# Turning the attention of a graph layer without TensorE: blocks of 32 on VectorE and a trip through DRAM

## The chip, the cores and the metric

The kernel runs on one core of a Trainium2 chip. The metric is the device time of one execution in microseconds (us). Before the change it is 2218.47 us, the median of three runs from 2218.12 to 2219.33 us. The profile is that of one execution with a span of 2214.6 us.

The engines that matter are TensorE (PE in the profile; PEld is its loading of weights), VectorE (DVE), ScalarE (ACT), GpSimd (POOL) and SyncE (SP), which here issues nearly all transfers. Each works through its own list of instructions in order, and waits on semaphores for the others.

## The reference

`x` has 128 batches of 128 nodes with 512 features, all float32. Four layers follow each other, each of the form `x = layernorm(x + layer(x))`. `adj` is a 128x128 weighted adjacency.

```python
# layer 0
y = einsum('nm,bmd->bnd', adj, x) @ weight + bias
# layer 1
rel = adj.T * (x Wq^T)(x Wk^T)^T
rel = rel / norm(rel, axis=2)
y = rel @ (x Wv^T)
# layer 2
h = x @ W
e = leaky_relu(s1[:, :, None] + s2[:, None, :], 0.2) * adj   # s1 = h a1, s2 = h a2
att = softmax(e, axis=2)
y = elu(att @ h + beta * h)
# layer 3
A = adj @ x;  C = adj @ x + b
y = max over the last axis of relu(A[:, :, None, :] + (C - A)[:, :, :, None])
```

The change concerns layer 2. There `att @ h + beta * h` is `(att + beta I) @ x @ W`, and this is how the kernel computes it: it needs the transpose of `att + beta I` as an operand of TensorE.

## The kernel before, in words

The 128 batches are worked in 32 groups (`NG`) of four (`G`). A tile of a group has 128 partitions (nodes) and 4x512 elements. Every matmul is in float32.

**Order of the work.** Each layer is cut into small pieces, and each piece is recorded with a due time by `emit(at, f)`. `TABLE` gives the due times of a group in slots; group g adds 28 slots for each group before it. At the end all pieces are sorted by due time and written out, and `InOrder` makes the framework keep this order on each engine. So four groups are in work at a time: while layer 2 of group g runs, layer 1 works on group g+1, layer 0 on group g+2, and the end of layer 2 and layer 3 on group g-1. `FIRST` and `LAST` give other times for the first two and the last three groups. Every instruction goes through the helper in line 26, so that the profile puts all of them on L26; they are told apart by their tiles.

**Products with weights.** The four products with 512x512 weights (tiles r_y, r_m, r_v, r_z for layers 0, 1, 1 and 2) are done as seven smaller products instead of eight, with sums of blocks. `product` emits them in the order 1, 2, 6, 5, 7, 3, 4, one slot apart, and for each an eviction 0.72 slots later. In the text they are called the first to the seventh product by this order. They share three regions of PSUM:

```python
ORDER = (1, 2, 6, 5, 7, 3, 4)
REGION = {1: 0, 6: 0, 7: 0, 4: 0, 2: 1, 5: 2, 3: 2}
```

A product that follows in the same region adds onto what stands there, after the earlier one has been read out. So the sixth product (number 3) waits for the eviction of the fourth (number 5), and the seventh (number 4) for that of the fifth (number 7). In layer 0 all seven evictions are VectorE additions onto x: `x<-r_y,x` in the profile.

**The attention of layer 2.** For a group: `spread` puts s2 along rows by TensorE, `leaky` adds s1 and applies the leaky ReLU on VectorE, `weighted` multiplies by `adj` on GpSimd, `greatest` takes the maximum on VectorE, `exps` does the exponentials with their sums on ScalarE. Then come the steps that the change touches:

- `divide` takes the reciprocals `rs` of the sums on VectorE, and multiplies the tile `e` (128 x 4 x 128) by them, on GpSimd where the whole group is done at once. In the last group, which goes batch by batch, it is on VectorE.
- `turn_att` turns the four 128x128 blocks on TensorE into the PSUM tile p_eT.
- `with_beta` adds beta times the identity (`beta_i`) on VectorE and writes the tile `eT`.
- `gather` multiplies x2 with `eT` on TensorE: p_z, copied to `zT` by ScalarE.

By the table `divide` is due at slot 65.8, `turn_att` at 68.6, `with_beta` at 69.0 and `gather` from 71.5 on. In the same slots VectorE has the fourth product's eviction of layer 0 for group g+2 (slot 66.72 in the count of group g), the variance `ve` of layer 2's norm of group g-1, its `nmean`, the fifth product's eviction, the masking of layer 1's scores (`rel`), and their turning in blocks (`relB`).

**Other turns without TensorE.** Layer 1 turns x (from group 2 on) and rel in blocks of 32x32 on VectorE (`turn_blocks`, `turn_rel`: tiles xB, relB) and then moves the blocks to their places by transfers from SBUF to SBUF, 16 a group each (`move`, `move_rel`: tiles xT, relT). They are all issued on SyncE's queue, in order, as are the loads of x and the stores of the result.

Of the kernel before, what the change touches and what calls it, by code (L numbers as in the profile page):

```python
# [8 lines left out]
FP = mybir.dt.float32  # L9
AF = mybir.ActivationFunctionType  # L10
ALU = mybir.AluOpType
# [18 lines left out]
def kernel(  # L30
# [33 lines left out]
    pe, dve, act, pool = (InOrder(tc, e) for e in (nc.tensor, nc.vector, nc.scalar, nc.gpsimd))  # L64
    sync = InOrder(tc, nc.sync)
    B, N, D = x.shape
    P = 128
    assert N == P and D % P == 0
    K = D // P
    Q = P // 32  # L70
    H = D // 2
    G = 4
    NG = B // G
# [4 lines left out]
    work = ctx.enter_context(tc.tile_pool(name="work", bufs=1))  # L78
    small = ctx.enter_context(tc.tile_pool(name="small", bufs=4))
    psum = ctx.enter_context(tc.tile_pool(name="psum", bufs=1, space=bass.MemoryType.PSUM))  # L80

    def bank(name):
        return psum.tile([P, D], FP, tag="ps", name=name, bufs=3)
# [56 lines left out]
    beta_i = const.tile([P, P], FP)  # L140
# [79 lines left out]
    def emit(at, f, *args):  # L220
        pieces.append((at, lambda: f(*args)))

    def each(at, f):
        for b in range(len(at)):
            emit(at[b], f, b)

    def row(at, step, n=G):
        return [at + i * step for i in range(n)]
# [6 lines left out]
        move=row(20.5, 0.1), x_sums=row(25.3, 0.5), m=row(28, 1, 7), scores=row(36.5, 1),  # L235
# [2 lines left out]
        residual=row(51.0, 1), dots=[51.7, 53.8, 54.9, 55.6], norm1=[54.6], scale=[57.2],  # L238
        apply1=row(65.4, 0.33),
        spread=[61.6], leaky=[62.0], weighted=[63.4], greatest=[64.3], exps=[64.4],  # L240
        divide=[65.8], turn_att=[68.6], with_beta=[69.0], gather=row(71.5, 1),
        z_sums=row(75.3, 0.5), z_w=row(77, 1, 7), exp=[87.5, 88.5, 90.4, 92.0],
        elu=[87.8, 89.4, 92.8, 93.8], norm2=[95.0], apply2=row(95.7, 0.33),
        widen=[98.7, 100.0, 103.6, 104.6], top=[99.1, 100.4, 104.0, 105.0],
# [14 lines left out]
            gather=row(36.7, 0.9), z_sums=row(39.95, 1.3),  # L259
# [6 lines left out]
            m=[0.0, 1.73, 3.46, 5.2, 7.4, 9.1, 10.8], scores=row(12.7, 0.9), masked=[16.4],  # L266
# [4 lines left out]
            turn_att=row(54.4, 0.6), with_beta=row(54.9, 0.6), gather=[55.2, 56.1, 60.5, 65.0],  # L271
# [98 lines left out]
    def rows_of(t):  # L370
        return lambda nh, ch: t()[:, 2 * nh : 2 * nh + 2, H * ch : H * ch + H]


    def stats(s, g, b, t):
        if b == 0:
            s["mv"] = small.tile([P, G, 2], FP, tag="mv", name=f"mv_{g}", bufs=6)
        st = small.tile([P, 6], FP, tag="st", name=f"st_{g}_{b}")
        dve.bn_stats(st, t)
        dve.bn_aggr(s["mv"][:, b, :], st)
# [239 lines left out]

    def layer2(g, t):  # L620
        s = {}

        def spread():
            s["p"] = bank(f"p_s2_{g}")
            for b in range(G):
                pe.transpose(
                    s["p"][:, b * P : (b + 1) * P],
                    s12[g][:, 1, b : b + 1].to_broadcast([P, P]),
                    ident,
                )  # L630

        def leaky():
            e = work.tile([P, G, P], FP, tag="e", name=f"e_{g}")
            dve.tensor_tensor(
                e,
                s["p"].rearrange("p (b n) -> p b n", b=G),
                s12[g][:, 0, :, None].to_broadcast([P, G, P]),
                ALU.add,
            )
            dve.scalar_tensor_tensor(e, e, ALPHA, e, op0=ALU.mult, op1=ALU.max)  # L640
            s["e"] = e

        def weighted():
            pool.tensor_tensor(s["e"], s["e"], adj_b, ALU.mult)

        def greatest():
            s["nm"] = small.tile([P, G], FP, tag="nm", name=f"nm_{g}")
            dve.tensor_reduce(s["nm"], s["e"], AX.X, ALU.max, negate=True)

        def exps(i):  # L650
            if i == 0:
                s["sums"] = small.tile([P, G], FP, tag="sums", name=f"sums_{g}")
            for b in range(i * n, i * n + n):
                act.activation(
                    s["e"][:, b, :],
                    s["e"][:, b, :],
                    AF.Exp,
                    bias=s["nm"][:, b : b + 1],
                    accum_out=s["sums"][:, b : b + 1],
                )  # L660

        def divide(i):
            rs = small.tile([P, n], FP, tag=f"rs{n}", name=f"rs_{g}_{i}")
            dve.reciprocal(rs, s["sums"][:, i * n : i * n + n])
            e = s["e"][:, i * n : i * n + n, :]
            engine = pool if n == G else dve
            engine.tensor_tensor(e, e, rs[:, :, None].to_broadcast([P, n, P]), ALU.mult)

        def turn_att(i):
            if i == 0:  # L670
                s["p"] = bank(f"p_eT_{g}")
            for b in range(i * n, i * n + n):
                pe.transpose(s["p"][:, b * P : (b + 1) * P], s["e"][:, b, :], ident)

        def with_beta(i):
            if i == 0:
                s["eT"] = work.tile([P, G, P], FP, tag="eT", name=f"eT_{g}")
            dve.tensor_tensor(
                s["eT"][:, i * n : i * n + n, :],
                s["p"].rearrange("p (b n) -> p b n", b=G)[:, i * n : i * n + n, :],  # L680
                beta_b[:, i * n : i * n + n, :],
                ALU.add,
            )

        def gather(b):
            if b == 0:
                s["zT"] = work.tile([P, K, G * P], FP, tag="aT_yz", name=f"zT_{g}")
            p = bank(f"p_z_{g}_{b}")
            for k in range(K):
                pe.matmul(  # L690
                    p[:, k * P : (k + 1) * P],
                    x2[g][:, b, k * P : (k + 1) * P],
                    s["eT"][:, b, :],
                    start=True,
                    stop=True,
                )
            act.copy(
                s["zT"][:, :, b * P : (b + 1) * P], p.rearrange("p (k n) -> p k n", k=K)
            )

        def begin():
            s["c"] = work.tile([P, G, D], FP, tag="c", name=f"c_{g}")
            for b in range(G):
                s["c", b] = s["c"][:, b, :]

        def direct(b):

            s["c", b] = psum.tile([P, D], FP, tag="r0", name=f"c_{g}_{b}", bufs=2)
            for k in range(K):
                pe.matmul(  # L710
                    s["c", b],
                    s["zT"][:, k, b * P : (b + 1) * P],
                    w2_sb[:, k, :],
                    start=(k == 0),
                    stop=(k == K - 1),
                )

        def exp(b):
            s["m", b] = work.tile([P, D], FP, tag="m", name=f"m_{g}_{b}", bufs=3)
            act.activation(s["m", b], s["c", b], AF.Exp)  # L720

        def elu(b):
            if b == 0:
                x3[g] = data.tile([P, G, D], FP, tag="x3", name=f"x3_{g}")
            x = x3[g][:, b, :]
            dve.scalar_tensor_tensor(
                x, s["c", b], 0.0, x2[g][:, b, :], op0=ALU.max, op1=ALU.add
            )
            dve.scalar_tensor_tensor(x, s["m", b], 1.0, x, op0=ALU.min, op1=ALU.add)
            stats(s, f"2_{g}", b, x)  # L730

        n = G // len(t["exps"])
        emit(t["spread"][0], spread)
        emit(t["leaky"][0], leaky)
        emit(t["weighted"][0], weighted)
        emit(t["greatest"][0], greatest)
        each(t["exps"], exps)
        each(t["divide"], divide)
        each(t["turn_att"], turn_att)
        each(t["with_beta"], with_beta)  # L740
        each(t["gather"], gather)
        if g < NG - 1:
            left_factors(t["z_sums"], s, "zT", "s_yz", f"z_{g}", 0)
            product(t["z_w"], f"z_{g}", by_rows, s, "2", rows_of(lambda: s["c"]), True, begin)
        else:
            each(t["z_w"], direct)
        each(t["exp"], exp)
        each(t["elu"], elu)
        norm(t["norm2"], t["apply2"], s, f"2_{g}", lambda: x3[g])
# [73 lines left out]
    for g in range(NG):  # L823
        for layer in (layer0, layer1, layer2, layer3):
            layer(g, times(g))
# [31 lines left out]
```

## Time and profile before

| what | value |
|---|---|
| time, median of 3 | 2218.47 us |
| span of the profiled execution | 2214.6 us |
| TensorE busy, matmuls | 2170.9 us (98%) |
| VectorE busy | 1547.9 us (70%) |
| ScalarE busy | 1102.5 us (50%) |
| GpSimd busy | 907.7 us (41%) |
| transpose of the attention on TensorE, p_eT | 128 instructions, 273 ns recorded each |
| adding beta, eT | 31 of 128x512, 674 ns each, and 4 of 128x128 |
| dividing on GpSimd, e by rs | 31, 1039 ns each |
| moves of rel, SBUF to SBUF | 512 issues, 16 KB each, 1.8 us to landing |

A busy time is the sum over an engine's instructions. Recorded matmuls overlap: the next begins before the record of the last ends, so the time that a matmul really holds TensorE is read from start to start, or from the chain of waits. On VectorE, too, an instruction that doesn't need the result of the one ahead starts a little before the record of that one ends. In a timeline a line has start, duration (both in us), engine, source line, operation, output and inputs; a bracket at its end gives how long the engine stood idle before it, and what released it.

### The profile page before, as it was taken

The page shows a single profiled execution, that of the slowest core. Times are in us where ns is not written, and L with a number is a line of the kernel's source. Part 1 is how long each engine was busy: PE and PEld are TensorE (multiplying, and loading weights), DVE is VectorE, ACT ScalarE, POOL GpSimd, SP SyncE. Part 2 cuts the span into 40 slices and gives each one's busy share as a digit, 9 for nine tenths or more (in the row PEclk, how much of TensorE's full clock was granted, in tenths as well). Part 3 has the DMA queues.
Part 4 walks back from the last instruction along what each step waited for, and adds up shares of the span by engine and source line. Part 5 has one row for each costly group of instructions (what it writes and reads, how often), then busy time and mean ns, then how long its engine had stood idle before and what let it go on. Part 6 is the DMA issues. An engine that isn't in the chain of part 4 may idle for free.

```text
span 2214.6 us, 31863 instructions
## 1 busy us (share of the span) xinstructions
PE 2170.9 (98%) x11073; PEld 1839.6 (83%) x11073; DVE 1547.9 (70%) x3290; ACT 1102.5 (50%) x2446; POOL 907.7 (41%) x743
## 2 busy tenths in 40 slices
PE   7999999999999999999999999999999999999996
PEld 5788888888888888888888888888888888888873
DVE  4657766767766767776767776767767677667676
ACT  2224445554445554445554445554455554455547
POOL 3334444334444344443344443344443344443321
PEclk9999999999999999999999999999999999999998
DMA  4011222211222211222112222112222112221101
GB/s 167 25 20 29 61 60 62 62 20 49 60 60 63 58 21 52 59 61 62 44 31 56 58 62 63 41 30 59 58 62 63 29 39 62 59 63 44 21 28 57
DMA packets 333295, 115.15 MB, mean 52 GB/s; under 512 B 297424, under 2 KB 297552, under 8 KB 333136
## 3 DMA queue, kind: packets, MB, share of 16 engines
q1 hardware_dynamic: 331936, 110.77, 19.7%
q10 hardware_dynamic: 1200, 2.36, 0.3%
q8 instruction: 88, 1.44, 0.3%
q14 instruction: 71, 0.58, 0.1%
HBM read 39.65 MB, written 33.55 MB: 33 GB/s over the span
## 4 chain that ended last, share of the span: by engine, by line
PE 93%; DVE 3%; ACT 2%; POOL 1%; issue 1%; DMA 0%; ACTq 0%; DVEq 0%; POOLq 0%
PE r_y L26 17%; PE r_v L26 17%; PE r_m L26 17%; PE r_z L26 17%; PE p_z L26 5%; PE p_rel L26 5%; PE p_y L26 5%; PE p_o L26 5%; PE p_a L26 5%; DVE x L26 1%; ACT x L26 1%; DVE st L26 1%; PE p_eT L26 1%; PE p_m L26 1%; PE p_s L26 1%
## 5 line engine op out<-in xcount | busy, mean ns | idle before, releaser
L26 ACT ACTIVATE x<-x,nmean,rstd 128x512 f32<-128x512 f32 x384 | 288.6, 808 | 120.8 <-DVE nmean L26 120.8
L26 DVE BATCH_NORM_STATS2 st<-x 128x6 f32<-128x512 f32 x384 | 263.8, 687 | 8.8
L26 POOL TENSOR_TENSOR x<-x,bias_sb 128x512 f32<-128x512 f32 x128 | 170.1, 1331 | 137.9 <-PE p_y L26 137.5
L26 DVE SCALAR_TENSOR_TENSOR x<-m,x 128x512 f32<-128x512 f32 x128 | 114.4, 894 | 108.5 <-ACT m L26 98.5
L26 POOL TENSOR_TENSOR s_x<-xT 128x512 f32<-128x512 f32 x64 | 82.2, 1285 | 261.1 <-DMA xT<-xB 250.2
L26 ACT COPY c<-r_z 128x512 f32<-128x512 f32 x124 | 71.2, 574 | 223.3 <-PE r_z L26 198.0
L26 ACT COPY yT<-p_y 128x512 f32<-128x512 f32 x128 | 75.1, 586 | 213.6 <-PE p_y L26 213.6
L26 POOL TENSOR_TENSOR rstd<-ve,mhalf 128x4 f32<-128x4 f32 (+1 forms) x99 | 98.5, 995 | 194.1 <-DVE ve L26 188.9
L26 DVE TENSOR_TENSOR x<-r_y,x 128x512 f32<-128x512 f32 x224 | 151.7, 678 | 31.2 <-PE r_y L26 31.0
L26 DVE SCALAR_TENSOR_TENSOR scr<-x,wa 128x512 f32<-128x512 f32 x256 | 161.5, 675 | 0.0
L26 DVE STREAM_TRANSPOSE xB<-x 128x512 f32<-128x512 f32 x120 | 81.2, 696 | 108.7 <-ACT x L26 97.7
L26 PEld LDWEIGHTS p_y<-adjT,x 128*128 128x128 f32 x1024 | 136.9, 196 | 11.2 <-ACT adjT L26 4.8
L26 POOL TENSOR_TENSOR s_z<-zT 128x512 f32<-128x512 f32 x31 | 39.4, 1270 | 255.9 <-ACT zT L26 255.9
L26 PE MATMUL p_y<-adjT,x 128*128 128x128 f32 x1024 | 137.6, 280 | 4.5 <-ACT adjT L26 4.5
L26 PEld LDWEIGHTS p_z<-eT,x 128*128 128x128 f32 x1024 | 134.0, 192 | 7.9 <-issue 1.0
L26 PEld LDWEIGHTS p_rel<-xT,tT 128*128 128x128 f32 x1024 | 134.1, 191 | 7.4 <-DVE tT L26 0.8
L26 DVE TENSOR_REDUCE mx<-p_a 128x1 f32<-128x512 f32 x128 | 88.3, 691 | 69.6 <-PE p_a L26 69.6
L26 PE MATMUL p_a<-x,adjT 128*128 128x512 f32 x256 | 130.8, 596 | 5.8 <-DVE mx L26 4.4
L26 ACT COPY tT<-r_m 128x512 f32<-128x512 f32 x128 | 75.6, 590 | 121.6 <-PE r_m L26 121.6
L26 PE MATMUL p_rel<-xT,tT 128*128 128x128 f32 x1024 | 134.9, 275 | 0.6 <-DVE tT L26 0.6
L26 PE MATMUL p_z<-eT,x 128*128 128x128 f32 x1024 | 134.7, 275 | 0.1
L26 PE MATMUL p_o<-v,relT 128*128 128x512 f32 x256 | 130.4, 593 | 0.3 <-ACT v L26 0.3
(129 smaller groups left out, 5268.6 us busy)
## 6 DMA issues: line engine op xcount, KB each, us to landing
out_dram<-x SPq DMA_DIRECT2D x128, 256.0 KB, 2.5
x<-in_x_dram SPq DMA_DIRECT2D x31, 1024.0 KB, 5.3
xT<-xB SPq DMA_DIRECT2D x480, 64.0 KB, 2.3
relT<-relB SPq DMA_DIRECT2D x512, 16.0 KB, 1.8
w_sb<-in_L_gnn_weight_dram ACTq DMA_DIRECT2D x1, 1024.0 KB, 5.6
x<-in_x_dram SPq DMA_DIRECT2D x4, 256.0 KB, 7.8
wq_sb<-in_L_gnn_Wq_dram SPq DMA_DIRECT2D x1, 1024.0 KB, 12.3
wk_sb<-in_L_gnn_Wk_dram SPq DMA_DIRECT2D x1, 1024.0 KB, 15.1
```

Source lines behind the costliest of these rows:

```text
L26: return lambda *args, **kw: self.tc.keep_in_program_order(op(*args, **kw))
```

## The change

For all groups but the last two, VectorE does the division and the addition of beta in one operation for each batch, `e = e * rs + beta_i`. Then it turns the whole tile in blocks of 32x32 by one operation (tile `eB`), a transfer writes that to a scratch tile in DRAM (`blocks`, 256 KB in rows of 2 KB), and four transfers read it back with the blocks in their places (`eT`, 64 KB each in pieces of 512 B). TensorE has no part in it any more, and neither p_eT nor GpSimd's multiplication remains. The last two groups go on as before. The purpose is to take the transposes from TensorE.

The new steps are due at slots 66.3 (`turn_blocks_2`) and 66.4 (`move_2`); the other times are the same. On VectorE the order in a group becomes: `rs`, four multiply-and-add steps, the turning into eB, then the fourth product's eviction and `ve` as before; the addition that wrote eT is gone. On SyncE's queue the write and the four reads of group g stand ahead of the moves of rel of group g+1; each read must wait for the write to have landed.

```diff
+    dram = ctx.enter_context(tc.tile_pool(name="dram", bufs=2, space=bass.MemoryType.DRAM))
...
-        divide=[65.8], turn_att=[68.6], with_beta=[69.0], gather=row(71.5, 1),
+        divide=[65.8], turn_att=[68.6], with_beta=[69.0], turn_blocks_2=[66.3], move_2=[66.4], gather=row(71.5, 1),
...
     def layer2(g, t):
         s = {}
+        late = g >= NG - 2
...
         def divide(i):
             rs = small.tile([P, n], FP, tag=f"rs{n}", name=f"rs_{g}_{i}")
             dve.reciprocal(rs, s["sums"][:, i * n : i * n + n])
+            if not late:
+                for b in range(G):
+                    e = s["e"][:, b, :]
+                    dve.scalar_tensor_tensor(
+                        e, e, rs[:, b : b + 1], beta_i, op0=ALU.mult, op1=ALU.add
+                    )
+                return
             e = s["e"][:, i * n : i * n + n, :]
...
+        def turn_blocks():
+            s["eB"] = work.tile([P, Q, G, P // Q], FP, tag="eB", name=f"eB_{g}")
+            dve.transpose(
+                s["eB"].rearrange("p q b u -> p b q u"),
+                s["e"].rearrange("p b (q u) -> p b q u", q=Q),
+            )
+
+        def move():
+            m = P // Q
+            blocks = dram.tile([P, Q, G * m], FP, tag="eB", name=f"eBd_{g}")
+            sync.dma_start(blocks, s["eB"].rearrange("p q b u -> p q (b u)"))
+            eT = work.tile([P, Q, G, m], FP, tag="eT", name=f"eT_{g}")
+            for q in range(Q):
+                sync.dma_start(
+                    eT[q * m : (q + 1) * m].rearrange("p a b u -> p a (b u)"),
+                    blocks.rearrange("(a j) q n -> q j a n", a=Q)[q],
+                )
+            s["eT"] = eT.rearrange("p a b u -> p b a u")
...
-        each(t["turn_att"], turn_att)
-        each(t["with_beta"], with_beta)
+        if late:
+            each(t["turn_att"], turn_att)
+            each(t["with_beta"], with_beta)
+        else:
+            emit(t["turn_blocks_2"][0], turn_blocks)
+            emit(t["move_2"][0], move)
```

## The prediction

> **What bounds the kernel now.** I read the page first, then the chain of waits of one group in the steady stretch, then the timelines of VectorE, GpSimd and TensorE over the same stretch, then the DMA list. All groups from the third on repeat the same picture, so one group stands for them.
>
> ```profile
> PE 2170.9 (98%) x11073; PEld 1839.6 (83%) x11073; DVE 1547.9 (70%) x3290; ACT 1102.5 (50%) x2446; POOL 907.7 (41%) x743
> PE 93%; DVE 3%; ACT 2%; POOL 1%; issue 1%; DMA 0%; ACTq 0%; DVEq 0%; POOLq 0%
> ```
>
> TensorE is nearly always busy, 93% of the chain runs over it, and the 40 slices show 9 tenths nearly throughout. Taking work from TensorE pays in full, as long as nothing else then holds it up. What the change takes away stands in the chain of waits (start, us, what):
>
> ```profile
> 1066.32 1.73 PE r_y L26 x8
> 1068.05 0.89 PE p_rel L26 x8
> 1068.94 1.73 PE r_y L26 x8
> 1070.67 0.44 PE p_eT L26 x4
> 1071.10 1.73 PE r_y L26 x8
> ```
>
> The four transposes p_eT hold TensorE for 0.44 us in each group, and nothing waits around them. The next group has the same line at 1070.67 - 1003.86 = 66.81 us before: that is the period. The three r_y lines are the fifth, sixth and seventh weight products of layer 0. The sixth adds onto the PSUM region that the fourth opened, the seventh onto that of the fifth, so each must wait until VectorE has taken out what stands there. VectorE at that time:
>
> ```profile
> 1063.81 0.68 DVE L26 TENSOR_TENSOR x<-r_y,x 128x512 f32<-128x512 f32 x1
> ...
> 1065.92 0.69 DVE L26 BATCH_NORM_STATS2 st<-x 128x6 f32<-128x512 f32 x1
> 1066.65 0.18 DVE L26 BATCH_NORM_AGGREGATE mv<-st 128x2 f32<-128x6 f32 x1
> 1066.75 0.14 DVE L26 RECIPROCAL rs<-sums 128x4 f32<-128x4 f32 x1
> 1066.81 0.66 DVE L26 TENSOR_TENSOR x<-r_y,x 128x512 f32<-128x512 f32 x1
> 1067.39 0.72 DVE L26 TENSOR_SCALAR ve<-mv 128x4 f32<-128x4 f32 x1
> 1069.23 0.16 DVE L26 SCALAR_TENSOR_TENSOR nmean<-mv,rstd 128x4 f32<-128x4 f32 x1 [1.13 <-POOL rstd L26]
> 1069.31 0.69 DVE L26 TENSOR_TENSOR x<-r_y,x 128x512 f32<-128x512 f32 x1
> ```
>
> The reader should see that VectorE, 70% busy over the span, has no gap here: from 1060.22 to 1068.11 it goes from one instruction to the next. The x<-r_y at 1066.81 takes out the fourth product and ends at 1067.47; TensorE starts the sixth at 1068.78 in its timeline (1068.94 in the chain, which dates a piece from the end of the one ahead). So 1.31 us are to spare. The x<-r_y at 1069.31 takes out the fifth and ends at 1070.00; the seventh starts at 1070.94: 0.94 us to spare. GpSimd:
>
> ```profile
> 1067.04 1.04 POOL L26 TENSOR_TENSOR e<-e,rs 128x512 f32<-128x512 f32 x1 [6.85 <-DVE rs L26]
> 1068.18 1.02 POOL L26 TENSOR_TENSOR rstd<-ve,mhalf 128x4 f32<-128x4 f32 x1
> ```
>
> **What the Trainium skill says.** "VectorE: DVE Perf Modes", section on the TRN2 errata, gives an fp32 two-input operation (N+151)/0.96 ns, 291 ns for N=128; the trace agrees (e<-e,rs of 128x128 in the last group: 291 to 293 ns). "SBUF — State Buffer", section Who interferes with whom, says VectorE and GpSimd share a port pair and the second to come is blocked. The trace agrees: ve of 128x4 takes 0.72 us, otherwise 0.16, and ends at 1068.11 when GpSimd's e<-e,rs ends at 1068.08. "DMA: Bandwidth & Descriptors", Two DMAs through the same engine are not ordered, says that a DMA that reads what another writes must wait for its semaphore; no run so far shows this pair, but the queue's order here has that wait.
>
> **The change part by part.** Thirty groups of 32 are changed.
>
> *Removed.* From TensorE 4 transposes, 0.44 us a group, on the path: 30 x 0.44 = 13.2 us. From GpSimd the multiply e<-e,rs, 1.04 us; GpSimd had been idle 6.85 us before it, so this gains nothing itself, but frees ve of its 0.56 us of blocking. From VectorE the addition eT<-p_eT,beta_i (0.67 us), which comes after the two critical evictions. The PSUM bank for p_eT is not asked for any more; TensorE waited for no bank, so nothing.
>
> *Added on VectorE*, between rs and the eviction of the fourth product: four SCALAR_TENSOR_TENSOR of 128x128 and one STREAM_TRANSPOSE of 128x512. The trace lacks the first at this size. Lower end: as the 128x128 additions, 0.29 us each and 0.08 less from start to start (0.68 recorded, 0.60 apart, on the 128x512 additions): 0.21. Upper end: with a column as scalar the 128x512 form takes 0.75 (x<-p_o,rn,x) instead of 0.68, so 0.36 and 0.28 apart. I take 0.31 and 0.24 apart: 3 x 0.24 + 0.31 = 1.03 us. The transpose has its like in xB<-x, 0.70, with 0.61 to the next start. Dependent steps start 0.03 after an end (AGGREGATE after STATS2). So: rs ends 1066.89; the four run 1066.92 to 1067.95; the transpose starts 1067.98; the fourth product's eviction starts 1068.59 instead of 1066.81, ends 1069.27. A matmul that waited for VectorE started 0.06 after it (125.61 against 125.55 in the second group), so the sixth starts at 1069.33, not 1068.78: 0.55 us late. All of the 1.31 us is used up. Restarted chains of 8 took 1.83 instead of 1.73, so TensorE is ready for the seventh at 1071.16.
>
> *Behind it.* ve starts 0.58 after the eviction, 1069.17, and takes 0.16; GpSimd's rstd starts 0.08 later, 1069.41 to 1070.43; nmean 1070.46; the fifth product's eviction 1070.54 to 1071.23; the seventh starts 1071.29 instead of 1070.94, and takes 0.10 more: TensorE leaves the place 0.45 us later than before, although it has 0.44 us less to do. Lower end 0.34 (4 x 0.03 less, and the last step shorter), upper 0.61. From there VectorE is even again: it has lost 1.23 us, and regains 0.6 by the missing addition eT, 0.17 and 0.28 in two idle gaps of its timeline by the next p_a. ScalarE gets nmean 1.23 us late and has gaps of 0.45 and 1.00 us before its copies of r_v matter. This repeats, as the start of the VectorE run (1052.95, released by TensorE's r_m) is tied to TensorE. In group 0 VectorE idles 1.85 us after rs, so there all is gain: -0.44. Sum: 29 x 0.45 - 0.44 = +12.6 us.
>
> *Added transfers.* eB is ready at about 1068.7. The write has the form of out_dram<-x (2.0 to 3.6 us to landing, median 2.5), the four reads that of adj_sb (64 KB in 512 B rows, 0.39 us to issue, 2.6 to land); issues on this queue take up to 0.6.
>
> ```profile
> out_dram<-x SPq DMA_DIRECT2D x128, 256.0 KB, 2.5
> xT<-xB SPq DMA_DIRECT2D x480, 64.0 KB, 2.3
> relT<-relB SPq DMA_DIRECT2D x512, 16.0 KB, 1.8
> ```
>
> Write landed 1071.2; last read issued 1072.5 to 1073.0; landed 1075 to 1076. The first p_z that needs it starts at 1076.98, now about 1077.4: hidden by 1.5 to 2.5 us. Behind the reads queue the 16 relT moves, ready at 1071.6; they start some 1.5 us late and end landing near 1086.5, against a first p_o near 1095: hidden. The queue is otherwise idle then.
>
> **The rivals.** (a) *The insertion fits*: VectorE's new steps are cheaper, or the evictions have more room than I read, and only the transposes count: 2218.5 - 13.2 = 2205.3. For it: TensorE at 98% and VectorE at 70%. Against: the order on VectorE, in which evictions stand behind the new steps, and 1.31 us to spare against 1.78 inserted. (b) *A draw*: the new steps cost some 0.35 us less than I take, gain and loss cancel: 2213 to 2222. (c) *The trip is late*: if write and reads take 3 us more, eT comes some 1 us after its p_z, and 30 x 1.1 us come on top of my sum: about 2264. For it: two receipts in a row. Against: an empty queue, and durations from the same trace.
>
> **How the numbers follow.** My forecast 0.70, (a) 0.15, (b) 0.10, (c) 0.05. Time: 2218.5 + 12.6 = 2231.1. My own ends, 0.34 and 0.61 a group, give 2228 and 2236. The range takes in (b) and the nearer part of (a), and above it some delay of the trip (0.3 us a group): 2209 to 2246. Faster by over 0.2%: (a) and a part of (b), 0.18; within: 0.08; slower: 0.74.
>
> **What would show it.** In the profile after, TensorE's idle time should name VectorE's x<-r_y as releaser ahead of r_y, in two places of each group, 0.4 to 0.6 and about 0.1 us; the four new steps should take 0.9 to 1.2 us together; ve should fall to 0.16; p_z should wait for no DMA; the period should be about 67.3. I am wrong if r_y doesn't wait and the period is 66.4, or if p_z waits for eT.

## The result, and the profile after

The changed kernel takes 2235.27 us (median of 4 runs, 2234.45 to 2236.53) against 2218.9 us for the kernel before (median of 4, 2218.12 to 2219.41): 16.4 us more, a ratio of 1.0075 with a 95% interval of 1.0057 to 1.0092. The forecast was 2231.1 us with a range of 2209 to 2246.

The page of the changed kernel: busy times, and the chain that ended last, by engine and by line.

```profile
PE 2171.7 (97%) x10953; PEld 1829.3 (82%) x10953; DVE 1562.4 (70%) x3410; ACT 1099.1 (49%) x2446; POOL 877.0 (39%) x713
PE 72%; DVE 21%; POOL 3%; issue 2%; ACT 1%; DMA 0%; DVEq 0%; ACTq 0%; POOLq 0%
```

The busy times hardly tell the two kernels apart. TensorE does 120 instructions fewer and is recorded as busy for as long: a matmul's record reaches past the start of the next, so part of a short wait, or all of it, is covered by the record ahead. The chain tells it: VectorE's share went from 3% to 21%, TensorE's from 93% to 72%. DMA stays at 0%.

The same place of the period in TensorE's timeline, first in the kernel before, from the scores (p_rel) ahead of the sixth product to the seventh:

```profile
1067.88 1.05 PE L26 MATMUL p_rel<-xT,tT 128*128 128x128 f32 x8
1068.78 1.89 PE L26 MATMUL r_y<-w_sb,s_y 128*128 128x256 f32 x8
1070.50 0.60 PE L26 MATMUL p_eT<-ident,e 128*128 128x128 f32 x4
1070.94 1.89 PE L26 MATMUL r_y<-t,yT 128*128 128x256 f32 x8
```

and in the changed kernel, with the product that comes next:

```profile
1075.96 1.05 PE L26 MATMUL p_rel<-xT,tT 128*128 128x128 f32 x8
1077.61 1.97 PE L26 MATMUL r_y<-w_sb,s_y 128*128 128x256 f32 x8 [0.60 <-DVE ve L26]
1079.49 1.99 PE L26 MATMUL r_y<-t,yT 128*128 128x256 f32 x8
1081.32 1.89 PE L26 MATMUL r_v<-wvT,xT 128*128 128x256 f32 x8
```

The p_eT line is gone, and a bracket has come: before the sixth product TensorE stands idle. From p_rel to the sixth product it is 1.65 us, where it was 0.90. The seventh starts 1.88 us after the sixth, where 1.73 is the undisturbed distance, and the next product 1.83 after that. The sixth product of the next group starts at 1145.00, so the period is 67.39 us instead of 66.81: 0.58 us more.

VectorE at that time:

```profile
1074.82 0.14 DVE L26 RECIPROCAL rs<-sums 128x4 f32<-128x4 f32 x1
1075.00 1.14 DVE L26 SCALAR_TENSOR_TENSOR e<-e,rs,beta_i 128x128 f32<-128x128 f32 x4
1076.17 0.71 DVE L26 STREAM_TRANSPOSE eB<-e 128x512 f32<-128x512 f32 x1
1076.81 0.65 DVE L26 TENSOR_TENSOR x<-r_y,x 128x512 f32<-128x512 f32 x1
1077.38 0.15 DVE L26 TENSOR_SCALAR ve<-mv 128x4 f32<-128x4 f32 x1
1078.66 0.16 DVE L26 SCALAR_TENSOR_TENSOR nmean<-mv,rstd 128x4 f32<-128x4 f32 x1 [1.13 <-POOL rstd L26]
1078.74 0.69 DVE L26 TENSOR_TENSOR x<-r_y,x 128x512 f32<-128x512 f32 x1
```

Count from the start of rs, which stands at the same place in both kernels (p_rel ahead of the sixth product starts 1.14 us after it, 1.13 before). The fourth product's eviction ends 2.64 us after it (0.72 before); the sixth product starts 2.79 after it (2.03 before). The fifth product's eviction ends 4.61 after it (3.25 before), and the seventh product starts 4.67 after it (4.19 before), 0.06 us after that eviction's end. The waits of the whole span (us in total, times, longest) say that this happens in 29 groups:

```profile
PE r_y L26 <- DVE ve L26: 17.3, 29, 0.6
PEld r_y L26 <- DVE x L26: 9.2, 29, 0.3
```

The first line names ve because it ended last ahead of the start. It was the eviction just before ve that let TensorE go: the trace has a separate wait instruction of TensorE there, which got through at 1077.50 us, when the eviction had been counted on VectorE's semaphore (1077.47) and ve had not yet (1077.55). The trip through DRAM, in SyncE's timeline:

```profile
1076.91 0.33 SPq L26 DMA_DIRECT2D eBd<-eB  x1
1078.93 1.74 SPq L26 DMA_DIRECT2D eT<-eBd  x4
1081.03 10.17 SPq L26 DMA_DIRECT2D relT<-relB  x16
```

The write lands after 2.0 us, and the reads are issued at once. With 2.0 us from issue to landing and the last issued about 1080.3, eT is complete near 1082.3. The first p_z starts at 1085.63: some 3.3 us to spare. Over the 30 groups it is 2.0 to 4.1 us. No p_z waits for a transfer.

### The profile page after: what moved, and what is told of

The parts are those of the page before. It is cut to its first block, busy times and chain, and to the rows that moved or that the text cites. A ratio compares the mean times of both kernels' runs of the same rounds, so it can differ in the third digit from the quotient of the medians.

```text
span 2233.3 us, 31980 instructions
## 1 busy us (share of the span) xinstructions
PE 2171.7 (97%) x10953; PEld 1829.3 (82%) x10953; DVE 1562.4 (70%) x3410; ACT 1099.1 (49%) x2446; POOL 877.0 (39%) x713
## 3 DMA queue, kind: packets, MB, share of 16 engines
q1 hardware_dynamic: 353536, 126.50, 21.7%
## 4 chain that ended last, share of the span: by engine, by line
PE 72%; DVE 21%; POOL 3%; issue 2%; ACT 1%; DMA 0%; DVEq 0%; ACTq 0%; POOLq 0%
PE r_v L26 17%; PE r_z L26 16%; PE r_m L26 12%; DVE x L26 10%; PE r_y L26 6%; PE p_z L26 5%; PE p_y L26 5%; PE p_o L26 5%; PE p_a L26 5%; DVE st L26 3%; DVE e L26 3%; DVE tT L26 2%; POOL e L26 2%; DVE eB L26 1%; ACT x L26 1%
## 5 line engine op out<-in xcount | busy, mean ns | idle before, releaser
L26 PE MATMUL r_y<-w_sb,s_y 128*128 128x256 f32 x512 | 123.2, 383 | 17.3 <-DVE ve L26 17.3
```

The source lines that it names most:

```text
L26: return lambda *args, **kw: self.tc.keep_in_program_order(op(*args, **kw))
```

## The experiments

Theory 1: the new VectorE steps push two evictions past the moments when TensorE wants their PSUM regions. Theory 2, the rival: the trip through DRAM, or the traffic that it adds (126.50 MB on SyncE's queue instead of 110.77), costs the time. All ratios are against the kernel before on the same chip, with 95% intervals. The changed kernel was not timed again beside these runs; the kernel before took 2218.51 us beside the first four and 2218.57 beside the last two, against 2218.9 above.

**The new steps left out** (division and beta are missing for the first 30 groups).

```diff
             if not late:
-                for b in range(G):
-                    e = s["e"][:, b, :]
-                    dve.scalar_tensor_tensor(
-                        e, e, rs[:, b : b + 1], beta_i, op0=ALU.mult, op1=ALU.add
-                    )
                 return
```

> The changed kernel without the four multiply-and-add steps (division and beta are left out for the first 30 groups; reciprocal, block turn, write and reads stay). Theory 1 (the new VectorE steps push the evictions of the fourth and fifth product past the moment when TensorE wants their PSUM regions): only the block turn's 0.65 us is left ahead of the fourth eviction, less than the 1.31 us to spare, so no wait of r_y is left and the 13.2 us of the transposes come out: 2205.7 us (2203 to 2209). Theory 2 (the trip through DRAM or its traffic costs the time): nothing of it is taken away, 2235 us.

Measured: 2205.86 us against 2218.51, ratio 0.9943 (0.9929 to 0.9958). In the waits of its whole span r_y stands behind one of its evictions once, for 0.3 us, instead of 29 times at two places. The whole trip with its traffic is in this kernel, and nearly the same room ahead of p_z (2.2 to 4.8 us); it is faster than the kernel before, so theory 2 can't hold.

**The transposes left out of the kernel before** (e goes to the gather unturned and without beta).

```diff
+        def as_it_is():
+            s["eT"] = s["e"]
+
...
-        each(t["turn_att"], turn_att)
-        each(t["with_beta"], with_beta)
+        if g < NG - 2:
+            emit(t["with_beta"][0], as_it_is)
+        else:
+            each(t["turn_att"], turn_att)
+            each(t["with_beta"], with_beta)
```

> The kernel before without the TensorE transposes and the VectorE addition of beta for the first 30 groups (e goes to the gather as it is: turn and beta are left out), and with nothing in their place. Both theories: the worth of the transposes by themselves, 30 x 0.44 = 13.2 us, 2205.7 us (2204 to 2208). If the time is 2215 or more, the transposes were not on the path and the sum in the prediction starts from a wrong term.

Measured: 2204.5 us (2203.45 to 2205.73), ratio 0.9937 (0.9922 to 0.9951): 14.0 us, about the 13.2 of the sum. The period is 66.37 us, 0.44 less than before. So the transposes were on the path with their full 0.44 us, and the changed kernel had that gain and lost some 30 us beside it.

**The steps moved behind the fourth eviction, and nmean behind the fifth.** Nothing is left out; only due times differ from the changed kernel.

```diff
-        divide=[65.8], turn_att=[68.6], with_beta=[69.0], turn_blocks_2=[66.3], move_2=[66.4], gather=row(71.5, 1),
+        divide=[66.8], turn_att=[68.6], with_beta=[69.0], turn_blocks_2=[66.85], move_2=[66.9], gather=row(71.5, 1),
...
-        elu=[87.8, 89.4, 92.8, 93.8], norm2=[95.0], apply2=row(95.7, 0.33),
+        elu=[87.8, 89.4, 92.8, 93.8], norm2=[95.0], apply2=row(95.85, 0.33),
```

> The changed kernel with other due times alone: the reciprocal, the four steps and the block turn come after the fourth product's eviction (divide 66.8, block turn 66.85, move 66.9), and nmean of the norm after the fifth product's eviction (apply2 from 95.85). Theory 1: the fourth eviction is as early as before; the fifth ends about 1070.1 in the time of the kernel before, TensorE wants it at 1070.5, so r_y waits nowhere and the transposes' gain comes out: 2205.7 us (2203 to 2210). eT lands about 1.5 us ahead of its first use. Theory 2: the trip starts 0.8 us later than in the changed kernel, so 2235 us or more.

Measured: 2205.56 us (2202.83 to 2205.91), ratio 0.9938 (0.9921 to 0.9954). It computes the same as the changed kernel with the same instructions and transfers, and beats both kernels, the changed one by about 30 us. Its VectorE timeline:

```profile
1062.70 0.66 DVE L26 TENSOR_TENSOR x<-r_y,x 128x512 f32<-128x512 f32 x1
1063.28 0.17 DVE L26 RECIPROCAL rs<-sums 128x4 f32<-128x4 f32 x1
1063.48 1.14 DVE L26 SCALAR_TENSOR_TENSOR e<-e,rs,beta_i 128x128 f32<-128x128 f32 x4
1064.65 0.71 DVE L26 STREAM_TRANSPOSE eB<-e 128x512 f32<-128x512 f32 x1
1065.29 0.13 DVE L26 TENSOR_SCALAR ve<-mv 128x4 f32<-128x4 f32 x1
1065.33 0.68 DVE L26 TENSOR_TENSOR x<-r_y,x 128x512 f32<-128x512 f32 x1
1066.55 0.16 DVE L26 SCALAR_TENSOR_TENSOR nmean<-mv,rstd 128x4 f32<-128x4 f32 x1 [0.54 <-POOL rstd L26]
```

and TensorE's:

```profile
1063.84 1.05 PE L26 MATMUL p_rel<-xT,tT 128*128 128x128 f32 x8
1064.73 1.89 PE L26 MATMUL r_y<-w_sb,s_y 128*128 128x256 f32 x8
1066.46 1.89 PE L26 MATMUL r_y<-t,yT 128*128 128x256 f32 x8
```

The steps take as long as in the changed kernel. But the fourth eviction ends at 1063.36, ahead of the sixth product at 1064.73, and the fifth at 1066.01, ahead of the seventh at 1066.46. No bracket stands in TensorE's lines, and the fifth eviction now uses time that VectorE had spent waiting for rstd. The period, taken from the start of the first product (1118.90 - 1052.53), is 66.37 us, 0.44 less than before. The trip starts later here, so eT lands only 1.1 to 1.8 us ahead of p_z, and still no p_z waits for it.

**Only the first of the two moves.** As above, but with apply2 left at 95.7, so that nmean stays ahead of the fifth eviction.

> As the run with both orders changed, but nmean stays ahead of the fifth product's eviction. Theory 1: the sixth product no longer waits, but now the steps delay ve, then GpSimd's rstd (1.02 us), nmean and the fifth eviction, which ends about 1071.4 where TensorE wants 1070.5 (time of the kernel before): the seventh product waits 0.9 us a group, less the 0.44 gained, some 0.5 to 0.6 net: 2233 to 2238 us, as slow as the changed kernel. If moving the steps behind the first eviction is enough (only one deadline matters), 2206 us. Theory 2: 2235 us or more, but with no wait at the seventh product.

Measured: 2233.51 us (2232.27 to 2236.72), ratio 1.0069 (1.0054 to 1.0084). VectorE and then TensorE:

```profile
1078.61 0.13 DVE L26 TENSOR_SCALAR ve<-mv 128x4 f32<-128x4 f32 x1
1079.87 0.16 DVE L26 SCALAR_TENSOR_TENSOR nmean<-mv,rstd 128x4 f32<-128x4 f32 x1 [1.13 <-POOL rstd L26]
1079.95 0.68 DVE L26 TENSOR_TENSOR x<-r_y,x 128x512 f32<-128x512 f32 x1
```

```profile
1078.05 1.89 PE L26 MATMUL r_y<-w_sb,s_y 128*128 128x256 f32 x8
1080.69 1.99 PE L26 MATMUL r_y<-t,yT 128*128 128x256 f32 x8 [0.74 <-DVE x L26]
```

The sixth product is on time, and the whole wait has moved to the seventh, which starts 0.06 us after the fifth eviction ends. The period is 67.39 us, as in the changed kernel. There are two deadlines, and meeting the first alone brings nothing: the same work is pushed through ve, rstd and nmean into the second. The other move alone, nmean behind the fifth eviction with the steps left ahead of the fourth, was not run.

**One more transfer in the trip, and two more.** The changed kernel, with eB first copied from SBUF to SBUF:

```diff
-            sync.dma_start(blocks, s["eB"].rearrange("p q b u -> p q (b u)"))
+            eC = work.tile([P, Q, G * m], FP, tag="eC", name=f"eC_{g}")
+            sync.dma_start(eC, s["eB"].rearrange("p q b u -> p q (b u)"))
+            sync.dma_start(blocks, eC)
```

> The changed kernel with one more transfer in the trip: eB is first copied from SBUF to SBUF (256 KB), then written to DRAM, then read. By the profile of the changed kernel the last read is issued about 1080.3 and lands about 1082.3, and the first p_z starts at 1085.63: 3.3 us to spare. One more hop costs about 2.1 us. Theory 1 (the trip is hidden): 2235 us (2232 to 2238), p_z waits for no DMA. Theory 2 (the trip costs the time): 30 x 2 us more, 2295 us.

Measured: 2233.7 us (2233.54 to 2235.53), ratio 1.0074 (1.0057 to 1.0091): the same as the changed kernel, though the trip is longer by a transfer of 2.4 us. About 1 us of the room is left in most groups. In a few late groups next to nothing is left, and p_z waits for eT once, for 0.2 us.

With two more, to DRAM and back before the write that was there:

```diff
-            sync.dma_start(blocks, s["eB"].rearrange("p q b u -> p q (b u)"))
+            first = dram.tile([P, Q, G * m], FP, tag="eA", name=f"eA_{g}")
+            sync.dma_start(first, s["eB"].rearrange("p q b u -> p q (b u)"))
+            eC = work.tile([P, Q, G * m], FP, tag="eC", name=f"eC_{g}")
+            sync.dma_start(eC, first)
+            sync.dma_start(blocks, eC)
```

> The changed kernel with two more transfers: written to DRAM, read back to SBUF, written to DRAM again, then read into its places. Two hops more cost about 4.2 us, 0.9 us more than the 3.3 to spare. Theory 1: the first p_z of each group waits for eT, 0.9 us and about 0.1 to restart, 30 times: 2235 + 30 = 2265 us (2250 to 2280). If it stays at 2235 the room is larger than the profile shows. Theory 2: 2355 us.

Measured: 2283.73 us (2280.22 to 2287.57), ratio 1.0297 (1.028 to 1.0314): 48.5 us above the changed kernel, beyond the range that was expected. In TensorE's timeline the wait is there:

```profile
1105.32 1.89 PE L26 MATMUL r_v<-wvT,xT 128*128 128x256 f32 x8
1108.45 1.13 PE L26 MATMUL p_z<-eT,x 128*128 128x128 f32 x8 [1.24 <-DMA eT<-eBd]
```

Without it p_z would start 1.73 us after the product ahead, at 1107.05; it is 1.40 us late here and 1.62 us in the next group, and the waits of the whole span have p_z behind eT 30 times. The read back into SBUF took 2.6 us and not 2.1, so the two hops added 2.0 + 2.6 = 4.6 us; less 1.4 to 1.6 leaves a room of 3.0 to 3.2 us, near the 3.3 read from the profile. So the room was about right, and the length of a hop, put at 2.1 us, was not.

## Why the prediction was right

The direction, the mechanism and the place were as forecast, and what it named as signs is in the profile: r_y waits for VectorE's evictions at two places of each of 29 groups (with 0.6 us of TensorE's idle time at the first), ve falls from 0.72 to 0.15 us, the four steps take 1.14 us together (0.9 to 1.2 forecast), p_z waits for no transfer, and the period is 67.39 us (67.3 forecast). By its steps:

- *Removed from TensorE, 13.2 us.* Right: 14.0 us where they and the addition of beta were left out, and 13.0 us net in the kernel with both moves.
- *Added on VectorE.* The mechanism was right, and two terms were too small. The four steps were put at 1.03 us and took 1.14, 346 ns recorded for one, near the upper bound. And TensorE was let start 0.06 us after the fourth eviction, but took 0.15. The sixth product came 0.76 us late and not 0.55.
- *Behind it.* ve, rstd, nmean and the fifth eviction followed each other as worked out; the fifth eviction ended 4.61 us after rs began, where 4.48 was forecast. TensorE left the place 0.58 us later than before instead of 0.45. This 0.13 us is the same 0.13 by which the fifth eviction ended later than forecast, and 0.11 of it is the four steps. The slower start of the sixth product, 0.15 us instead of 0.06, added nothing, because the seventh waits for the fifth eviction in any case. It only made that second wait shorter: some 0.05 us, if the sixth takes the 1.83 us of a restarted chain, where 0.13 was forecast. With 0.58 in the sum, 29 x 0.58 - 0.44 = 16.4 us, which is what was measured. That it fits to 0.1 us is luck: the four runs of either kernel differ by 1 to 2 us among themselves, and the spans of the two profiled executions differ by 18.7.
- *Regained later.* Right: VectorE waits 0.28 us for the next p_a in both kernels, so it is even again by then, and the period is longer by the 0.58 us of this place alone.
- *Added transfers hidden.* Right, with more room than forecast: 3.3 us instead of 1.5 to 2.5, as the write landed in 2.0 us and the reads in 2.0.
- *Rivals.* (a), that the insertion fits, is false for the order that was chosen and true for another order of the same steps. (b), a draw, needed steps 0.35 us shorter than the sum had, and they were 0.11 longer. (c) was brought about only by two more hops.

What isn't settled is why the sixth product takes 0.15 us. That its weights were not loaded ahead doesn't set it apart, as those of the seventh weren't either. The separate wait instruction does, but no run takes it away.

## What to carry to other kernels

An engine at 70% can still have no room where it matters: list its instructions between the new work and the next thing that the bound engine waits for, and compare what is inserted with what is to spare (here 1.31 and 0.94 us). Put new work behind the urgent evictions rather than ahead, and follow each later deadline too: one move alone left 2233.5 us, the two together gave 2205.6. The latency of the transfers here cost nothing while their room lasted (one more hop, 2233.7 us), and once it was used up each group lost what was missing (two more hops, 1.4 to 1.6 us a group).

## What the runs showed of the hardware that was not expected

- TensorE restarts at two different distances from the end of a VectorE eviction. The sixth product has a separate wait instruction ahead of it; its weights begin to load at 1077.58, after the eviction's end at 1077.46, and it starts at 1077.61, 0.15 us after that end. The weight load of the seventh carries the wait itself; it begins at 1079.49, and the product with it, 0.06 us after the eviction's end at 1079.43. Both distances are the same in all 29 groups. In the run with two more hops p_z, also behind a separate wait instruction, starts 0.13 to 0.14 us after the landing of eT.
- A 128x128 multiply-and-add with a column and a tile as operands takes 346 ns on VectorE, where the 128x128 addition takes 291.
- A write of 256 KB to DRAM in 2 KB rows landed in 2.0 us in all 30 groups of the changed kernel (2.0 to 3.2 in the run with one more hop), and a 64 KB read in 512 B pieces in 2.0 in the median; the read of 256 KB back into SBUF took 2.6.
